# Two chunks' scores, then two chunks' sums, then products: another order of TensorE's work in a fused attention and expert layer

## The chip, the cores and the metric

The kernel runs on one core of one Trainium2 chip. The metric is the device time of one execution in microseconds (us). The kernel before took 775.37 us, the median of three runs (775.12 to 777.02).

The engines are named as in the profile: PE is TensorE (matrix products), PEld its weight loads, DVE is VectorE, ACT is ScalarE, POOL is GpSimd, SP issues most DMAs.

## What is computed

The input is x of 4 sequences (B) of 1024 positions (T) with 256 channels (C), all in float32. Two residual layers follow each other:

```python
x = x + attention(layernorm(x))   # 16 heads of 16, causal, with a slope per head (ALiBi)
x = x + ffn(layernorm(x))
```

The attention scores are `q @ k.T / 4 + slope * (key - query)` for keys up to the query, softmax over the keys, times v, then a projection. The second layer is, for each position, a small attention over the 4 sequences of the batch (16 heads of 16), a projection, a layer norm, a router that takes the higher number of the two best of 8 experts, that expert's two products with a GELU in between, and another layer norm.

## The kernel before

**Units, groups, rounds.** The attention works on units: a sequence with a chunk of 256 queries (chunks 0 to 2, twelve units), and a sequence with 128 queries for the last chunk (eight units: its first halves for all sequences, then its second halves). `begins` (L2147) says at which place each unit begins; `begins[B]`, the first unit behind the first chunk, is 8. A unit has 4 groups of 4 heads, and the keys of a group are taken in rounds of up to 512 columns (key block by queries). A round that holds the diagonal is narrower where keys are later than queries: 384 columns for the own round of a 256-query unit, and for the first halves of the last chunk, where the second round has three key blocks of four.

**A round** is scored by `score` (L986), later weighed by `weigh` (L1023). `score` multiplies keys by queries, 4 heads at once, in TensorE tiles of 32 rows (the profile's `sk<-slots`, 32*128); the result lies in two pairs of PSUM banks, two heads each. ScalarE takes the exp of each pair (L1007, `p<-sk`), so two exps to a round, into tiles of the pool `probs`, which has 7. The own round is then masked by GpSimd (L1017). `weigh` takes two rounds and multiplies values by these tiles, 4 heads at once, in tiles of 32 columns (`pv<-p,v`, 128*32), into one more pair of banks, which ScalarE copies out or VectorE adds to what is there (L1063, L1065). It also gives the sums of the softmax, by a column of ones, which is why the text calls this step "sums".

**PSUM.** There are four pairs of banks. `pair_of_banks` (L663) gives them out in turn: whatever takes a pair waits until the one that took it four calls earlier has been read. `bank` (L669) gives a single bank: a fresh pair's first half, then its second half, unless `pair_of_banks` was called in between.

**Products** are all other work of TensorE, in tiles of 128*128: transposes of the normalised input and projections to q, k and v of later units (`xtp`, `qkp`, `vp`), projections of finished units (`op`), and the second layer's products (`utp`, `qkvp`, `ctp`, `ao`, `place`) of fronts. A front (L1594) is a generator of the second layer for 128 positions of the 4 sequences; its stages are marked D (products), E, P (VectorE), N (ScalarE), R (GpSimd).

**Places.** The order of everything is written out by the loop at L2302. Rounds are taken by twos; a place p holds rounds 2p and 2p+1 and there are 80 places. In each, in this order: the first round's score; `E_slot` (L2248: work due at this half place, stores, loads, then the fronts' VectorE stages); `D_slot` (L2260: products due at this place, then fronts' products up to an estimated 10 us, with VectorE stages in between); `fill` (L2298: the loads of keys for a unit's group into `slots`, once the unit before is scored); more VectorE stages; the second round's score; `weigh` of the two rounds of the place before (`waiting`); `fill`; `E_slot` again. A planner keeps estimates of the time of each engine (`time`) and of each pair (`pair_free`), and lets a front's stage go only when it should be ready, so its estimates choose which place a product falls in. [...]

`at_E` puts work at a half place, `at_D` at a place. `prepare_biases` (L1488) splits biases into three bfloat16 pieces and stores each by a DMA; its last stage needs what `prepare_router(2)` leaves behind at place 11 (L2244).

Of the kernel before, what the change touches and what calls it, by code (L numbers as in the profile page):

```python
# [38 lines left out]
B, T, C = 4, 1024, 256  # L39
# [568 lines left out]
def fast_layer(ctx: ExitStack, tc: tile.TileContext, odd, x, wq, wk, wv, wp, w_in, w_out, w_r,  # L608
# [252 lines left out]
    sums, at = [], 0  # L861
# [13 lines left out]
    def issue_stores(*keys, age=None):  # L875
        due = [it for it in stores if it[0] in keys or age is not None and it[1] >= age]
        for it in due:
            stores.remove(it)
            it[2]()
# [77 lines left out]
    def fill_slots(u, g):  # L957

        n, i, _ = units[u]
        c, b = batches[n]  # L960
        if b == 0 and c and i == 0:
            query_rows(c, g)
        n_cols = W + (c + 1) * W
        issue_stores(("k", n, g // 2))
        src = k_of[b][4 * g * D:4 * (g + 1) * D, :n_cols]
        if c == 0:
            row_ = 4 * (g % 2) * D
            src = held["kq", n, g // 2][row_:row_ + 4 * D].rearrange("p k w -> p (k w)")
        queue = nc.scalar if u == 0 and g % 2 else nc.sync
        queue.dma_start(slots[g][0:P:2, :n_cols], src)  # L970
# [11 lines left out]
    def n_rounds(u):  # L982
        n, i, size = units[u]
        return -(-(batches[n][0] * PC + i + size) // (QC // (size * P)))
# [150 lines left out]
    for j in range(4):  # L1135
        at = slice(j * S, (j + 1) * S)
# [351 lines left out]
    def prepare_biases(stage):  # L1488

        if stage == 0:
            b1_rows = fact.tile([E, C], F32, tag="equal", name="b1_rows")
            nc.scalar.dma_start(
                b1_rows.rearrange("e (c p) -> e c p", p=P),
                b1.rearrange("p (e c) -> e c p", c=CC),
            )
            b2_rows = fact.tile([E, C], F32, tag="before", name="b2_rows")
            nc.scalar.dma_start(b2_rows, b2)
            b_row = fact.tile([1, 2 * C], F32, tag="u", name="b_row", bufs=2)  # L1500
            for k, at in enumerate((B_IN, B_OUT)):
                nc.scalar.dma_start(
                    b_row[:, k * C:(k + 1) * C], rows[at:at + C].unsqueeze(0)
                )
            held["biases"] = (
                (b1_rows, b_bf[0]), (b2_rows, b_bf[1]),
                (b_row[:, :C], in_bf), (b_row[:, C:], out_bf),
            )
            return
        src, three = held["biases"][stage - 1]  # L1510
        if three is out_bf:
            nc.vector.tensor_tensor(src, src, router["passed"][0:1, :C], ALU.add)
        n, width = src.shape
        rest = fact.tile([n, width], F32, tag="pr", name="rest")
        nc.vector.tensor_copy(rest, src)
        pieces = fact.tile([n, 3, width], BF16, tag="turned", name="pieces", bufs=TURNED)
        for k in range(3):
            nc.vector.tensor_copy(pieces[:, k], rest)
            nc.sync.dma_start(three[k * n:(k + 1) * n, :width], pieces[:, k])
            if k < 2:  # L1520
                nc.vector.tensor_tensor(rest, rest, pieces[:, k], ALU.subtract)
# [545 lines left out]
    def load_next():  # L2067
        while to_load and (
            to_load[0] < X_BUFS or left_x[(to_load[0] - X_BUFS) // B] == PC
        ):  # L2070
            load_x(to_load.pop(0))
# [5 lines left out]
    def busy(on, cost, ready=0.0):  # L2077
        time[on] = max(time[on], ready) + cost
        return time[on]

    def on_tensor(cost):
        return busy("PE", cost, max([0.0] + [pair_free[k] for k in taken]))
# [6 lines left out]
    def product(cost, what):  # L2089
        taken.clear()  # L2090
        what()
        end = on_tensor(cost)
        busy("DVE", OF_D * cost, end - 0.5 * cost)
        read_at(max(end + READ, time["DVE"]))
        return end

    def start_fronts():
        if queue and len(running) < 2:
            issue_stores(*[it[0] for it in stores if it[0][0] == "u"])
        while queue and len(running) < 2:  # L2100
            running.append(Running(queue.pop(0)))

    def take_E(some=True):

        start_fronts()
        left = some
        while left:
            left = False
            for it in list(running):
                now, kind = time["PE"], it.kind  # L2110
                if kind not in ("E", "N", "R", "P"):
                    continue
                on = {"E": "DVE", "P": "DVE", "N": "ACT"}.get(kind)
                if it.ready > max(now, time[on] if on else 0.0) + EARLY_BY:
                    continue
                if on == "DVE" and time["DVE"] > now + AHEAD:
                    continue
                if kind == "R":
                    it.ready = max(now, it.ready) + ROOT
                else:  # L2120
                    it.ready = busy(on, it.cost if on == "DVE" else 0.5, it.ready)
                left = True
                it.next()
                if it.kind == "end":
                    running.remove(it)

    def take_D(cost, some):

        for it in list(running):
            while it.kind[0] in "Dd":  # L2130
                if it.kind == "DQ" and ("qkv",) in held:
                    break
                if it.kind != "d" and it.ready > time["PE"] + EARLY_BY:
                    break
                if cost and cost + it.cost > D_SLOT:
                    break
                if it.kind == "DQ":
                    held["qkv",] = True
                cost += it.cost
                end = product(it.cost, it.next)  # L2140

                it.ready = max(end + READ, time["DVE"])
                take_E(some)
            if it.kind == "end" and it in running:
                running.remove(it)

    begins = [0]  # L2147
# [4 lines left out]
    def at_E(k, what, cost=0.0):  # L2152
        of_E.setdefault(k, []).append((cost, what))
# [7 lines left out]
    for u, (n, i, size) in enumerate(units):  # L2161
# [4 lines left out]
        if u == n:  # L2166
            if n > 2:
                at_E(2 * begins[n - 3], lambda n=n: to_load.append(n))
            for k in range(3):
                at = (-5, -5, -4)[k] if n == 1 else 2 * q - 7 + k  # L2170
# [37 lines left out]
    def pop_due(due, now):  # L2208
        some = sorted((it for it in due if it[0] <= now), key=lambda it: it[0])
        for it in some:  # L2210
            due.remove(it)
        return [(cost, what) for _, cost, what in some]
# [24 lines left out]
        at_E(1 + g, lambda g=g: key_rows(g, W, T, nc.vector if g else nc.gpsimd))  # L2237
    at_E(4, prepare)
    at_E(6, part.prepare)
    for k, at in enumerate((-6, 12, 13, 14, 23)):  # L2240
        at_E(at, lambda k=k: prepare_biases(k))
    at_D(9, 1.0, lambda: prepare_router(0))
    at_D(10, 1.5, lambda: prepare_router(1))
# [4 lines left out]
    def E_slot(k, some=True):  # L2248
        for cost, what in of_E.pop(k, []) + pop_due(due_E, time["PE"]):
            what()  # L2250
            busy("DVE", cost)
        issue_stores(age=1)
        for it in stores:
            it[1] += 1
        load_next()
        if tables and fetching:
            experts.fetch()
        take_E(some)

    def D_slot(p, some=True):  # L2260
        todo = of_D.pop(p, []) + pop_due(due_D, time["PE"])
        for cost, what in todo:
            product(cost, what)
        take_D(sum(cost for cost, _ in todo), some)
# [11 lines left out]
    def columns_of(u, r):  # L2276
        return sum(units[u][2] * P - off for _, off in blocks_of(u, r))

    def score_next(k):
        u, g, r = rounds[k]  # L2280
        taken.clear()
        waiting.append((u, g, r, score(u, g, r)))
        end, n = on_tensor(SWITCH + columns_of(u, r) * COLUMN), columns_of(u, r)
        for pair in list(taken):
            pair_free[pair] = busy("ACT", EXP_AT_ALL + 2 * n * EXP, end)
        if r == n_rounds(u) - 1 and u < last_unit:
            to_fill.append((u + 1, g))
# [10 lines left out]
    def fill():  # L2298
        while to_fill:
            fill_slots(*to_fill.pop(0))  # L2300

    for p in range(len(rounds) // 2):  # L2302
        then = p < len(rounds) // 2 - 1
        score_next(2 * p)
        E_slot(2 * p)
        D_slot(p, then)
        fill()
        take_E(then)
        score_next(2 * p + 1)
        if len(waiting) > 2:  # L2310
            weigh_next(waiting[:2])
            del waiting[:2]
        fill()
        E_slot(2 * p + 1, then)
    for _, what in pop_due(due_E, NEVER):
        what()
    weigh_next(waiting)
# [105 lines left out]
    while threads:  # L2423
# [4 lines left out]
        at, _, it = min((begin(it) + FIRST_BY * n, n, it) for n, it in enumerate(threads))  # L2428
# [124 lines left out]
```

## Time and profile before

| what | value |
|---|---|
| median of three runs | 775.37 us |
| the profiled execution | 776.72 us, of which the span from first to last instruction 774.9 us |
| granted clock of TensorE, mean | 0.97 |
| scoring: matmul records, busy | 3456, 178.5 us |
| weighing: matmul records, busy | 3456, 146.9 us |
| exps of scores: count, mean of one | 320 x 128 partitions, 940 ns |

A float32 product appears as two records. The loop of places runs from about 21 to 606 us, places 8 and up from about 78 us; the experts follow.

Further views that bear on the change are the waits of TensorE from 78 to 600 us: 4.5 us for VectorE's copies of `kq` (4 times), 4.0 us of the weighing for ScalarE's exps (11 times), 3.7 us of the scoring for exps (7 times), 3.5 us of `place` for VectorE (3 times). A row of such a view says who waited, for whom, the sum, how often and the longest. A row of the timeline says when a group of like instructions began, how long it lasted from its first start to its last end, engine, line, operation, output<-inputs, the shape, how many, and in brackets how long the engine stood before it and what ended that. Line 589 is a helper through which TensorE, VectorE and ScalarE are called, so groups are told apart by their tiles.

### The profile page before, as it was taken

How to read it: one execution, taken by the hardware profiler on the slowest of the kernel's cores; microseconds unless marked ns; L12 is line 12 of the kernel's file. 1: busy time of each engine (PE TensorE's matmuls, PEld its weight loads, DVE VectorE, ACT ScalarE, POOL GpSimd, SP SyncE). 2: the span in 40 equal slices, each digit the busy share in tenths (PEclk: the TensorE clock that was granted, in tenths of full speed). 3: DMA queues.
4: the chain of work that ended last, by engine and by line, in shares of the span. 5: the costliest groups of instructions: out<-in, count | busy, mean ns of one | idle time of the engine just before them, and what ended most of it. 6: DMA issues, size and time to landing. Idle time of an engine off the chain costs nothing. (4 is left out here: it accounts for less than half of the span.)

```text
span 774.9 us, 21884 instructions
## 1 busy us (share of the span) xinstructions
PE 696.7 (90%) x8945; PEld 525.6 (68%) x8945; DVE 514.0 (66%) x1266; ACT 425.9 (55%) x647; POOL 243.0 (31%) x345
## 2 busy tenths in 40 slices
PE   3989899999999999999989999999999687989991
PEld 2667577666666666575668877687778456878891
DVE  5447436477985765899672427698679778877462
ACT  1545547555465656556557656568558054546550
POOL 4644113221222221104221221123112330478873
PEclk9999999999999999999999999999999898999996
DMA  7535544431452432315354445345342670344421
GB/s 227 167 117 176 172 129 139 139 118 49 129 160 86 140 113 67 102 58 159 93 172 134 142 146 164 93 139 187 112 116 58 174 282 1 110 137 128 125 82 41
DMA packets 70872, 98.48 MB, mean 127 GB/s; under 512 B 15408, under 2 KB 54635, under 8 KB 70252
## 3 DMA queue, kind: packets, MB, share of 16 engines
q1 hardware_dynamic: 58528, 67.82, 28.4%
q10 hardware_dynamic: 7884, 16.05, 6.6%
q0 software_dynamic: 4352, 13.11, 5.6%
q8 instruction: 74, 1.21, 0.6%
q14 instruction: 34, 0.28, 0.1%
HBM read 60.50 MB, written 34.59 MB: 123 GB/s over the span
## 5 line engine op out<-in xcount | busy, mean ns | idle before, releaser
L589 ACT ACTIVATE p<-sk 128x1024 f32<-128x1024 f32 (+1 forms) x320 | 287.9, 940 | 148.4 <-PE sk L589 118.6
L1017 POOL TENSOR_SCALAR_AFFINE_SELECT p<-p 128x512 f32<-128x512 f32 (+1 forms) x160 | 106.6, 670 | 404.8 <-ACT p L589 402.5
L589 PE MATMUL sk<-slots 32*128 32x128 f32 (+1 forms) x3456 | 178.5, 325 | 10.1 <-DVE kq L589 4.7
L589 PEld LDWEIGHTS sk<-slots 32*128 32x128 f32 x3456 | 134.6, 187 | 53.5 <-issue 20.5
L589 PE MATMUL pv<-p,v 128*32 128x128 f32 (+1 forms) x3456 | 146.9, 317 | 9.6 <-ACT p L589 4.0
L589 PEld LDWEIGHTS pv<-p,v 128*32 128x32 f32 x3456 | 96.9, 111 | 48.8 <-issue 10.0
L589 PE MATMUL qkvp<-w_in,ut 128*128 128x264 f32 (+1 forms) x240 | 83.5, 486 | 0.2 <-ACT ut L589 0.2
L589 PEld LDWEIGHTS qkvp<-w_in,ut 128*128 128x128 f32 x240 | 42.5, 190 | 28.8 <-issue 24.3
L589 PE MATMUL qkp<-xt,wqk 128*128 128x256 f32 x224 | 56.4, 397 | 0.0
L589 DVE COPY kq<-qkp 128x512 f32<-128x512 f32 x28 | 19.1, 684 | 50.1 <-PE qkp L589 50.1
L589 PEld LDWEIGHTS qkp<-xt,wqk 128*128 128x128 f32 x224 | 41.5, 194 | 10.7 <-issue 3.3
L589 PE MATMUL hid<-mt,w 128*128 128x128 f32 x272 | 41.4, 289 | 2.6 <-ACT ge L589 1.7
L589 ACT ACTIVATE mt<-mtp,columns 128x128 f32<-128x128 f32 x68 | 27.4, 454 | 26.9 <-PE mtp L589 26.9
L589 ACT COPY qkv<-qkvp 128x512 f32<-128x512 f32 x28 | 16.4, 585 | 44.9 <-PE qkvp L589 44.7
L589 DVE TENSOR_TENSOR pv<-vr,sc 128x1024 f32<-128x1024 f32 x32 | 39.2, 1224 | 2.4 <-PE ctp L589 2.1
L1868 POOL DMA_INDIRECT given<-rows,rows x34 | 37.4, 1100 | 9.0 <-issue 7.9
L589 DVE COPY vr<-qkvp 128x264 f32<-128x264 f32 x28 | 12.1, 431 | 42.1 <-PE qkvp L589 42.1
L589 PEld LDWEIGHTS hid<-mt,w 128*128 128x128 f32 x272 | 37.2, 198 | 3.9 <-ACT ge L589 2.2
L589 DVE TENSOR_REDUCE sc<-pr 128x64 f32<-128x1024 f32 x32 | 39.0, 1220 | 1.1
L589 DVE TENSOR_TENSOR pr<-qkv 128x1024 f32<-128x1024 f32 x32 | 39.2, 1224 | 0.5 <-ACT qkv L589 0.2
L1983 POOL DMA_INDIRECT out_dram<-o,out_rows x34 | 34.6, 1018 | 7.4 <-issue 5.0
L589 PE MATMUL oe<-w,ge 128*128 (+1 forms) x136 | 36.8, 395 | 0.0
(320 smaller groups left out, 1005.1 us busy)
## 6 DMA issues: line engine op xcount, KB each, us to landing
slots<-k SPq DMA_DIRECT2D x32, 320.0 KB
k<-kq SPq DMA_DIRECT2D x32, 256.0 KB
v<-v ACTq DMA_DIRECT2D x4, 1152.0 KB
x<-in_x_dram SPq DMA_DIRECT2D x16, 256.0 KB
y<-yt SPq DMA_DIRECT2D x16, 256.0 KB
rows<-x SPq DMA_DIRECT2D x32, 128.0 KB
slots<-k SPq DMA_DIRECT2D x16, 256.0 KB
rows<-u SPq DMA_DIRECT2D x8, 512.0 KB
```

What stands on the lines that cost most here:

```text
L589: ins = made(*args, **kwargs)
L1017: nc.gpsimd.affine_select(blocks, blocks, pattern=[[0, 2], [0, size], [1, P]], compare_op=ALU.is_ge, fill=0.0, base=0, channel_multiplier=-1,)
L1868: nc.gpsimd.indirect_dma_start(out=self.hx, out_offset=None, in_=t.rows_of, in_offset=bass.IndirectOffsetOnAxis(ap=t.rows_[:, self.j:self. ...
L1983: ins = nc.gpsimd.indirect_dma_start(out=out.rearrange("t n c -> (t n) c"), out_offset=bass.IndirectOffsetOnAxis(ap=t.table.out_rows[:, t. ...
```

## The change

From place 8 on (`between` is false) the order in a place is: first score, `fill`, `E_slot`, second score, `fill`, `weigh`, `E_slot`, `D_slot`, VectorE stages. In places 0 to 7 the order stays. The last stage of `prepare_biases` moves from half place 23 to 25, since place 11's products now come behind both its half places.

```diff
-    for k, at in enumerate((-6, 12, 13, 14, 23)):
+    for k, at in enumerate((-6, 12, 13, 14, 25)):
         at_E(at, lambda k=k: prepare_biases(k))
...
     for p in range(len(rounds) // 2):
         then = p < len(rounds) // 2 - 1
+        between = p < begins[B]
         score_next(2 * p)
+        if not between:
+            fill()
         E_slot(2 * p)
-        D_slot(p, then)
-        fill()
-        take_E(then)
+        if between:
+            D_slot(p)
+            fill()
+            take_E()
         score_next(2 * p + 1)
+        if not between:
+            fill()
         if len(waiting) > 2:
             weigh_next(waiting[:2])
             del waiting[:2]
-        fill()
+        if between:
+            fill()
         E_slot(2 * p + 1, then)
+        if not between:
+            D_slot(p, then)
+            take_E(then)
```

## The prediction, made before the changed kernel was run

> **What bounds the kernel now.** I read the engine rows first, then busy time by stretch, then who waited for whom on TensorE, and last the timeline of TensorE.
>
> ```profile
> PE 696.7 (90%) x8945; PEld 525.6 (68%) x8945; DVE 514.0 (66%) x1266; ACT 425.9 (55%) x647; POOL 243.0 (31%) x345
> ...
> 78.00:190.00 112.00, 108.35 (x1088) 74.76 (x1084) 60.34 (x132) 60.87 (x88) 24.13 (x32) 0.98 0.41 126
> 190.00:390.00 200.00, 191.04 (x2127) 128.37 (x2119) 153.42 (x344) 117.83 (x156) 44.33 (x49) 0.98 0.35 108
> 390.00:505.00 115.00, 109.94 (x2053) 86.51 (x2053) 59.42 (x141) 70.65 (x101) 22.31 (x39) 0.99 0.47 144
> 505.00:600.00 95.00, 90.80 (x2082) 74.84 (x2075) 79.42 (x193) 65.48 (x84) 21.06 (x35) 1.00 0.40 123
> ```
>
> From 78 to 600 us, which is nearly all that the change touches, TensorE works some 96% of the time; VectorE reaches 77% in the second stretch and 84% in the fourth, ScalarE at most 69%. So in the attention part the order of instructions on TensorE sets the time, and each gap on it counts in full. The clock column (0.98 to 1.00) stays out of it. The remaining 175 us (experts) hold none of the reordered loop.
>
> One stretch of TensorE's timeline shows both kinds of place side by side:
>
> ```profile
> 417.74 1.84 PE L589 MATMUL sk<-slots 32*128 32x128 f32 x56
> ...
> 419.00 3.35 ACT L589 ACTIVATE p<-sk 128x1024 f32<-128x1024 f32 x4 [0.79 <-PE sk L589]
> 420.08 1.74 PE L589 MATMUL pv<-p,v 128*32 128x128 f32 x56 [0.50 <-ACT p L589]
> ...
> 421.75 1.17 PE L589 MATMUL sk<-slots 32*128 32x128 f32 x32
> ...
> 422.85 1.99 PE L589 MATMUL qkp<-xt,wqk 128*128 128x256 f32 x8
> ...
> 424.77 0.95 PE L589 MATMUL sk<-slots 32*128 32x128 f32 x24
> ...
> 425.65 1.74 PE L589 MATMUL pv<-p,v 128*32 128x128 f32 x56
> ...
> 427.32 1.17 PE L589 MATMUL sk<-slots 32*128 32x128 f32 x32
> ```
>
> sk is scoring, pv weighing, all else (here qkp) a product. At 421.75 stands a place as today: first score, product, second score, sums. At 417.74 stands a place with **no product due**: its scores (32+24 records) already run back to back, then the sums. That is exactly the order that the change gives to every place, so before already shows its price: the sums start 2.34 us after the first score (417.74 to 420.08), with TensorE idle for 0.50 us because ScalarE has not yet emptied the first pair of banks. The cause is in the code. There are four pairs, taken in turn. Two scores take all four, so weigh() gets the first score's first pair again and must wait for its exp: that starts 1.26 us after the score (419.00) and takes about 0.97 us. With a product in between, weigh() gets the product's pair, or one further on.
>
> **The sum, part by part.** Counting the places from 8 on (72 of the 80) in TensorE's timeline: 59 have products, 13 have none. These 13 keep their order and cost what they cost now.
>
> *Scores and sums (the path).* First score plus second score, start to next start, in places without a stall: 1.08+0.87 = 1.95 us in the second chunk (512 score columns, then 384), 1.10+0.88 = 1.98 in the fourth chunk's first half, 1.10+1.10 = 2.20 in its second half (512, 512). After, by the places that have no product: 2.32, 2.34 and 2.34. In the third chunk all three pairings occur: 512/384 goes from 1.95 to 2.32; 512/512 from 2.16 to 2.32; 384/512 from 1.95 to about 1.96 (an exp over 768 starts 1.05 us after its score and takes 0.81; with 0.1 us to the sums, 1.96). Times the counts:
> second chunk 15 x 0.37 = 5.6; third 8 x 0.37 + 5 x 0.16 + 8 x 0.01 = 3.9; fourth 12 x 0.36 + 11 x 0.14 = 5.9. **Together +15.4 us.** The saving in tilings is already inside these differences.
>
> *Tilings, and two rules.* The Trainium skill, "TensorEngine Tiling (Array Packing)", Key Properties, says that changing the tiling mode drains TensorE. The trace agrees: the 56 score records start in groups of four 0.112 us apart, so 14 groups are 1.56 us and 8 are 0.89, where the 8 groups from 421.75 take 1.10: 0.21 us for entering and leaving. By that rule alone two scores in one block save about 0.2 us: 59 x 0.2 = 12 us gained. The same page, PSUM Bottleneck, speaks against the change: tiling speeds up TensorE, not the emptying of PSUM, which may become the limit. Here it does: the two scores could be followed at about 1.79 us, and the exp allows 2.34. I take the row, +15.4. The switch from sums straight to a product is nowhere in before; leaving the sums for a score costs 1.67 - 14 x 0.109 = 0.14 us. Between 0 and twice this, 59 places move by -8 to +8; I take it unchanged.
>
> *Stalls that vanish.* Where the product is tiny, the second score stands today for the exp of the first, four times (235, 370, 577, 597 us) or is pulled apart by the switch (526): against 2.2 their score pairs cost 0.7 to 1.8 more. Two scores in a row do not have these waits: **-5 us**.
>
> *Products end directly before two scores.* The last pair of a product is needed again four pairs later. Today that is the next place's first score, after a score and the sums, 2.7 us behind the product. After, it is the next place's second score, 0.9 us behind it (1.3 us before it costs anything, as the sums wait anyway). VectorE empties most products, in order behind the fronts' work:
>
> ```profile
> 403.57 0.19 DVE L589 TENSOR_TENSOR hot<-low_con,expert 128x32 bf16<-128x32 f32 x1
> 403.68 0.68 DVE L589 COPY kq<-qkp 128x512 f32<-128x512 f32 x1
> ...
> 404.42 0.93 PE L589 MATMUL sk<-slots 32*128 32x128 f32 x16 [2.10 <-DVE kq L589]
> ```
>
> Here the product ended at 399.70 and was copied out by 404.36, 4.7 us late. Reading the end of the last copy of every product in the timeline: 21 of the 59 end more than 1.3 us after it, in sum 27 us over. Some 9.5 us of such waits exist today, so with the same lateness +17 us; if the longer places give VectorE the time to catch up, 0. Its queue is fed after the sums as it is fed today after the first score, so nothing makes it earlier, but a wait on TensorE drains it: I take the middle, **+8**.
>
> *The rest.* take_E and E_slot are called as often as before, so VectorE's and GpSimd's work is the same in number. An exp of a front (`sc<-sc`) waiting for VectorE holds ScalarE's queue ahead of the score's exp, which is now on the path: six or seven fronts, under 0.5 us each, **+2**. fill() moves ahead of E_slot and D_slot: 60 loads of slots (0.49 us of SP each), the stores of k that they push out, and query_rows at two chunk ends (0.35 + 0.41 us of VectorE, eight times) are issued 1 to 5 us earlier; on SP they already wait for scores, and the rows are read four or more places (over 20 us) later: 0, or some 3 us if VectorE stands for a score. The last biases (three small DMAs on SP, six VectorE operations) go from half place 23 to 25, one place after the product they need; first used near 208 us, they are there by 125: 0. Fronts get further while the places are longer, which may take **-1 us** from the tail.
>
> Sum: 15.4 - 5 + 8 + 2 - 1 = +19 us on the profiled execution's 776.7 us (span 774.9 and 1.8 around it), 796. The median, 775.4, lies 1.3 lower: **794 us**. A measurement of this kernel tells 0.3% (2.3 us) from no change.
>
> **Rivals.**
> 1. *The tiling decides* (faster): if the exp's wait were hidden, a place would go from 1.98 to 1.79 us: 59 x 0.19 = -11, 764 us. For it: the drain is real, and a free switch from sums to product adds to it. Against it: 13 of 13 places without a product show the wait. It decides only if the wait stays under 0.19 us, or if the waits standing today around products (score pairs 20 us over their base, sums 9.5) vanish by more than the 15.4. Chance 0.09.
> 2. *Gains and waits cancel*: 15.4, less 5 of vanishing stalls, less 8 for a free switch into the products: +2, 777 us, with late copies at 0. Needs three terms at one end. Chance of within 0.3%: 0.04.
> 3. *VectorE's copies become the bound*: lateness unchanged (+17), a dearer switch (+8): 15.4 + 17 + 8 + 2 - 5 = +37, 813 us. For it: VectorE at 77% in the third chunk (190 to 390 us), where most late copies lie. Against it: a standing TensorE lets that queue run empty. Chance of more than 810: 0.07.
> The forecast, slower by 4 to 35 us, holds 0.80. That the order does not change is excluded: the pairs go by the order of calls.
>
> **How the numbers follow.** Range 779 to 810: +4 is the sum with the switch at its low end and late copies at 1; +35 is rival 3 nearly whole. Below lie 0.13 (rivals 1 and 2), above 0.07. Faster 0.09, same 0.04, slower 0.87.
>
> **What would show it.** In the profile after: TensorE's wait of sums for p by ScalarE rises from 4 us in 11 cases (78 to 600 us) to some 20 to 30 us in over 50; first score to sums 2.3 us in places with a product too; PE's busy time about equal and its share lower; waits of the second score for VectorE's kq, vr, u or ct. Wrong, if sums start less than 2 us after a full first score, or if a switch into products is far from 0.14 us.

## The result, and the profile after

The changed kernel takes **805.8 us** (median of 4 runs, 805.36 to 807.25), where the kernel before takes 775.75 us beside it (4 runs): ratio **1.0383** [1.0356, 1.041], slower by about 30 us. The profiled execution has a span of 803.4 us, against 774.9.

The engine rows of the page after (busy time, share of the span, instructions), then TensorE's waits from 78 to 600 us (who waited for whom: us in all, times, longest):

```profile
PE 695.7 (87%) x8945; PEld 535.0 (67%) x8945; DVE 511.5 (64%) x1266; ACT 417.4 (52%) x647; POOL 236.1 (29%) x345
```

```profile
PE pv L589 <- ACT p L589: 22.6, 44, 3.2
PE sk L589 <- DVE x L589: 6.3, 3, 2.8
PE qkp L589 <- DVE ctx L589: 3.4, 2, 3.2
```

TensorE has the same number of instructions and the same busy time as before (695.7 and 696.7 us), and a span 28.5 us longer. The weighing's wait for ScalarE's exps, 4.0 us in 11 cases before, is now 22.6 in 44 (20 to 30 us in over 50 cases were forecast). Busy time by stretch (TensorE first, in us; then PEld, DVE, ACT, POOL; the granted clock; DMA share; GB/s) shows that in the loop the clock is not it, and that TensorE's share fell in each stretch:

```profile
78.00:190.00 112.00, 102.70 (x1046) 73.44 (x1038) 56.97 (x131) 55.89 (x84) 22.32 (x31) 0.97 0.40 123
190.00:390.00 200.00, 182.43 (x1995) 127.43 (x1997) 154.50 (x341) 107.76 (x146) 38.81 (x46) 0.98 0.34 106
390.00:505.00 115.00, 107.13 (x1931) 82.89 (x1925) 56.36 (x139) 68.83 (x99) 20.37 (x37) 1.00 0.45 142
505.00:600.00 95.00, 89.90 (x2033) 73.87 (x2032) 68.52 (x181) 62.86 (x83) 19.20 (x35) 1.00 0.41 129
```

TensorE's timeline after, at one place with a product in front of it:

```profile
427.64 1.03 PE L589 MATMUL qkp<-xt,wqk 128*128 128x256 f32 x4
...
428.60 1.84 PE L589 MATMUL sk<-slots 32*128 32x128 f32 x56
...
429.87 3.35 ACT L589 ACTIVATE p<-sk 128x1024 f32<-128x1024 f32 x4 [2.43 <-PE sk L589]
...
430.94 1.74 PE L589 MATMUL pv<-p,v 128*32 128x128 f32 x56 [0.50 <-ACT p L589]
```

The product (qkp) stands ahead of the two scores, the scores run as one block of 56 records, and the sums begin 2.34 us after the first score (428.60 to 430.94) having stood 0.50 us for the exp: the row that the prediction took from a place without a product, now in a place with one.

**Where the 28.5 us are.** I cut the trace at three points: the start of the last sums of the loop, and the first and the last matmul of `counts_all`, the count of tokens for each expert, behind which the bulk of the experts' work stands in TensorE's order. The count has five matmuls: one adds the fronts up to front 6 (`so_far`), four add front 7 (`hot`).

| stretch | before | after | difference |
|---|---|---|---|
| start to last sums | 603.5 | 620.6 | +17.1 |
| last sums to the count's first matmul | 72.9 | 83.9 | +11.0 |
| first matmul to the count done | 0.3 | 7.6 | +7.3 |
| count done to end | 98.2 | 91.3 | -6.9 |

The loop costs about what was forecast. The +11.4 us behind it were not foreseen. These rows of TensorE's timeline are of before (first fence) and after (second), from the last sums to the count:

```profile
603.51 1.96 PE L589 MATMUL pv<-p,v 128*32 128x128 f32 x64 [2.39 <-DVE yn L589]
...
615.03 1.72 PE L589 MATMUL ctp<-ident,ctx 128*128 128x128 f32 x8
...
631.37 0.19 PE L589 MATMUL place<-hot,lower 128*128 128x32 bf16 x1 [1.40 <-DVE hot L589]
...
676.41 0.17 PE L589 MATMUL counts_all<-so_far,ones_bf 128*128 128x8 bf16 x1
676.44 0.24 PE L589 MATMUL counts_all<-hot,ones_bf 128*128 128x8 bf16 x4
```

```profile
620.63 1.95 PE L589 MATMUL pv<-p,v 128*32 128x128 f32 x64
...
640.36 0.52 PE L589 MATMUL ctp<-ident,ctx 128*128 128x128 f32 x3
...
689.15 0.18 PE L589 MATMUL place<-hot,lower 128*128 128x32 bf16 x1
...
704.54 0.17 PE L589 MATMUL counts_all<-so_far,ones_bf 128*128 128x8 bf16 x1
711.88 0.25 PE L589 MATMUL counts_all<-hot,ones_bf 128*128 128x8 bf16 x4 [7.17 <-DVE hot L589]
```

`ctp` and `place` here belong to front 6, the last front that begins inside the loop (the last front of all, 7, runs behind it). Counted from the last sums, its transposes of the context stand at +11.5 us before and +19.7 after, and its `place` at +27.9 and +68.5: after, it is served so late that work of experts and of front 7 comes between. The count begins 11 us later, then stands 7.17 us for front 7's `hot` on VectorE, and is done 18.3 us later (73.2 and 91.5 us behind the last sums). Part of this comes back: between the last sums and the count TensorE has done 11 of the experts' pieces (one piece is a tile of tokens through its expert's two products, about 2.7 us of TensorE) instead of 7, so 23 instead of 27 are left behind it, and the part behind it is 6.9 us shorter. The net is the +11.4.

### The profile page after: what moved, and what is told of

Its sections match the earlier page's. It is cut to its first block, busy times and chain, and to the rows that moved or that the text cites. A ratio compares the mean times of both kernels' runs of the same rounds, so it can differ in the third digit from the quotient of the medians.

```text
span 803.4 us, 21919 instructions
## 1 busy us (share of the span) xinstructions
PE 695.7 (87%) x8945; PEld 535.0 (67%) x8945; DVE 511.5 (64%) x1266; ACT 417.4 (52%) x647; POOL 236.1 (29%) x345
## 5 line engine op out<-in xcount | busy, mean ns | idle before, releaser
L589 ACT ACTIVATE p<-sk 128x1024 f32<-128x1024 f32 (+1 forms) x320 | 277.7, 943 | 154.9 <-PE sk L589 135.6
L1017 POOL TENSOR_SCALAR_AFFINE_SELECT p<-p 128x512 f32<-128x512 f32 (+1 forms) x160 | 100.9, 634 | 437.1 <-ACT p L589 435.2
L589 PE MATMUL sk<-slots 32*128 32x128 f32 (+1 forms) x3456 | 168.2, 322 | 15.5 <-DVE x L589 6.3
L589 PEld LDWEIGHTS sk<-slots 32*128 32x128 f32 x3456 | 138.2, 188 | 46.8 <-issue 13.3
L589 PEld LDWEIGHTS pv<-p,v 128*32 128x32 f32 x3456 | 98.7, 112 | 65.3 <-ACT p L589 28.5
L589 PE MATMUL qkvp<-w_in,ut 128*128 128x264 f32 (+1 forms) x224 | 77.5, 483 | 0.0
L589 PEld LDWEIGHTS qkvp<-w_in,ut 128*128 128x128 f32 x224 | 40.5, 193 | 26.9 <-issue 22.6
L1868 POOL DMA_INDIRECT given<-rows,rows x34 | 38.0, 1118 | 21.8 <-DVE at_t L589 12.8
L589 ACT COPY qkv<-qkvp 128x512 f32<-128x512 f32 x24 | 14.1, 587 | 50.4 <-PE qkvp L589 50.4
```

What stands on the lines that cost most here:

```text
L589: ins = made(*args, **kwargs)
L1017: nc.gpsimd.affine_select(blocks, blocks, pattern=[[0, 2], [0, size], [1, P]], compare_op=ALU.is_ge, fill=0.0, base=0, channel_multiplier=-1,)
L1868: nc.gpsimd.indirect_dma_start(out=self.hx, out_offset=None, in_=t.rows_of, in_offset=bass.IndirectOffsetOnAxis(ap=t.rows_[:, self.j:self. ...
```

## The experiments

Two theories were to be tested. **Loop:** the sums stand for the exp of the first score's first pair, in the places from 8 on. **Tail:** where front 6 stands when the loop ends. The table has every run in the order of the text: its median with the ratio to the kernel before in the same set of runs, and four readings of its own trace: when the last sums start, and the time from there to the first matmul of the count, to the count done, and to the end. The kernel before itself has medians of 775.75, 786.84, 782.27, 776.75 and 776.46 us in the five sets, so times are compared by ratio, and places in the loop by trace.

| run | median, us | ratio | last sums | to the count | count done | to the end |
|---|---|---|---|---|---|---|
| before (the first profile) | 775.75 | 1 | 603.5 | 72.9 | 73.2 | 171.4 |
| after (the first profile) | 805.8 | 1.0383 [1.0356, 1.041] | 620.6 | 83.9 | 91.5 | 182.8 |
| e5_new_until_48 | 797.19 | 1.0096 [1.006, 1.0132] | 616.1 | 72.4 | 72.7 | 180.7 |
| e6_new_from_48 | 796.92 | 1.0115 [1.006, 1.017] | 612.7 | 83.8 | 91.4 | 184.6 |
| e12_new_until_64 | 807.71 | 1.039 [1.0344, 1.0436] | 623.9 | 84.5 | 92.1 | 184.0 |
| e1_after_early | 808.55 | 1.0268 [1.024, 1.0296] | 629.7 | 78.9 | 79.2 | 180.9 |
| e2_before_early | 793.89 | 1.0092 [1.0059, 1.0125] | 608.4 | 74.6 | 74.9 | 185.2 |
| e7_after_again | 806.32 | 1.0293 [1.0235, 1.0352] | 620.6 | 84.9 | 92.5 | 184.6 |
| e8_before_again (one run) | 782.5 | | 601.4 | 70.8 | 71.0 | 179.1 |
| e3_after_split | 811.31 | 1.0355 [1.0276, 1.0433] | 625.5 | 85.0 | 92.6 | 185.0 |
| e4_before_split | 785.18 | 1.0033 [1.0, 1.0066] | 604.8 | 72.3 | 72.6 | 176.9 |
| e9_after_short | 815.0 | 1.0485 [1.045, 1.052] | 609.3 | 83.5 | 91.1 | 204.1 |
| e10_before_short | 795.92 | 1.0253 [1.0214, 1.0291] | 601.2 | 72.2 | 72.5 | 192.1 |
| e11_before_sums_first | 786.46 | 1.0131 [1.0105, 1.0157] | 614.0 | 71.6 | 71.9 | 170.6 |

### Which chunk makes the tail

The new order for a part of the places. The edit in the changed kernel, for the second and third chunk alone (e5), and for the fourth chunk alone (e6):

```diff
-        between = p < begins[B]
+        between = p < begins[B] or p >= begins[3 * B]      # e5
+        between = p < begins[3 * B]                        # e6
```

> The new order in places 8 to 47 alone (second and third chunk), the old one from 48. Theory (the loop loses by the first score's exp, 9.5 us in these two chunks; the 11 us behind the loop are lost because the front that begins last in the loop stands further back when it ends, which the fourth chunk's order sets): 775.4 + 9.5 + 1 = 786 us, and from the last sums to the end 171 us as before. Rival (any new order costs the tail its 11 us): 797 us, 183 us behind the loop.

> The new order from place 48 on alone (fourth chunk). Theory: the loop loses 5.9 us and about 1 us of late copies, the tail 11 us: 793 us, with 182 to 183 us behind the last sums. Rival (the tail's loss goes with the loop's total delay, of which this is a third): 775.4 + 7 + 4 = 786 us.

The loop's loss splits: last sums at 616.1 and 612.7 us, 12.6 and 9.2 later than before, 21.8 together against 17.1 for both at once. The count does not split. In e5 it is done 72.7 us behind the last sums, as in the kernel before (7 pieces of the experts ahead of it); in e6 91.4, as in the changed kernel (11 pieces). So the late count comes with the order in the fourth chunk, and a longer loop by itself does not bring it: e5's is 12.6 us longer.

The whole time behind the last sums, by which both forecasts were stated, fits less well: 180.7 us in e5, nearer to its rival's 183 than to the theory's 171, and 184.6 in e6. e5's excess lies behind the count (108.0 us, before 98.2), and e8 below, the kernel before itself, has it too (108.1). By ratio the halves cost 1.0% and 1.2%, together less than the changed kernel's 3 to 4%. e5's 1.0% is nearer to the theory (786 of 775.4 us, 1.4%) than to its rival (2.8%), but e6's 1.2% is nearer to its rival (1.4%) than to the theory (2.3%). So the two halves show where the late count comes from, not what it costs.

### What in the fourth chunk: its last places, or where front 6 stands

In the emitted order, front 6 takes its stage in front of `qkvp` at place 73 before, and at place 75 after. It cannot begin until unit 15 is projected; that projection runs at 540.7 us before and 559.3 after. The planner dates it by the end of unit 15's weighing, which its estimates put 13.5 us later in the new order, and the new order asks for the products due only behind both scores and the sums of a place. The following kernel separates this from what happens in the last places themselves: these run in the old order, but the planner still lets front 6 go late, at place 76.

```diff
-        between = p < begins[B]
+        between = p < begins[B] or p >= begins[3 * B] + 16
```

> The changed kernel with the new order for the places 8 to 63 only; the last 16 places run in the old one. In the emitted order of this kernel, front 6 (the last that begins in the loop) begins its matmuls with wqk's successors at place 76 of 80, against 75 in the changed kernel and 73 in the kernel before, because the sums of unit 15 fall 13.5 us later in the planner's time as in the changed kernel. Theory (the 11 us behind the loop come from where front 6 stands in the instruction streams, not from the order within the last places): from the last sums to the experts' count it takes 80 to 88 us, as in the changed kernel (84), although the last 16 places have the old order. Rival (the order within the last places leaves VectorE with more work at the loop's end): 71 to 74 us, as in the kernel before. Loop by the counts of the prediction: new order costs all but the fourth chunk's second half, so the last sums start at 615 to 620 us.

The last 16 places have the old order, and to the count it is still 84.5 us (done at 92.1):

```profile
620.53 5.39 PE L589 MATMUL pv<-p,v 128*32 128x128 f32 x128
...
699.05 0.19 PE L589 MATMUL place<-hot,lower 128*128 128x32 bf16 x1 [0.98 <-DVE hot L589]
...
708.40 0.17 PE L589 MATMUL counts_all<-so_far,ones_bf 128*128 128x8 bf16 x1
715.75 0.25 PE L589 MATMUL counts_all<-hot,ones_bf 128*128 128x8 bf16 x4 [7.18 <-DVE hot L589]
```

Front 6's `place` comes even later (75.1 us behind the start of the last sums, 623.9, which lies inside the first row's group) and the count with it, with the same wait of 7.18 us in it. The theory holds for the count, and its rival falls. The forecast of the loop, 615 to 620 us, was missed by 4: the places 64 to 79 took 105.9 us in the old order, 102.9 in the changed kernel.

### Bringing front 6 forward

Unit 15's sums, reciprocals and projection are made due sooner, in the changed kernel (e1) and in the kernel before (e2):

```diff
                 by = HURRIED.get(by, NEVER)
+            if u == (NC * B) - 1:
+                by = {SUMS_BY: 2.0, INVERTED_BY: 5.5, Y_BY: 7.5, DIVIDED_BY: 14.0}[by]
             due_E.append((at + by, cost, lambda what=what: what(u)))
         by = NEVER if u == last_unit - 1 else PROJECTED_BY
+        if u == (NC * B) - 1:
+            by = 15.0
```

> The changed kernel, but the last first-half unit (15) of the fourth chunk is divided and projected 14 and 15 us of the planner's time behind its sums instead of 26 and 28, so that the front that waits for it begins earlier. Theory (that front's unfinished stages cost the tail its 11 us): its transposes begin in the loop some 10 us earlier, the time behind the last sums falls from 183 to about 172 us, the whole to 795 us. Rival (the tail is longer for another reason, such as a later last unit): 804 to 806 us.

> The kernel before, with the same earlier division and projection of unit 15. Theory (the stage of that front at the loop's end sets the tail): it gains here too, since two of its four last weighted sums and its norm stand in the tail today: 3 to 8 us, 767 to 772 us. Rival (in the old order the last front and the experts alone set the tail): 775 us, no change.

In the changed kernel the count is done 79.2 us behind the last sums instead of 91.5, and front 6's `place` moves from +68.5 to +30.9: the count follows front 6, by 12 of the 18 us. The time to the end hardly does: 180.9 us behind the last sums, where the theory said about 172 and the rival 183, and where the changed kernel has 182.8 and 184.6. And the loop pays: the last sums start at 629.7, 9 us later. In the kernel before nothing is gained at all (count done at 74.9 against 73.2, loop 5 us longer), and that expectation was missed too: a front's work has to be done somewhere, and inside the loop it stands in front of scores. The planner's dates are a balance that moving one of them did not improve.

### The same two kernels again

Both unchanged, on the chip of e3 and e4 (that of the first profiles is not on record), to see which readings repeat. e8 is a single run; its 782.5 us lie close to the 782.27 of the kernel before in its set.

> The changed kernel as it is, for a trace on the chip of the other runs of this call. 1.038 of the kernel before; the last sums at 620 us, 83 to 84 us from them to the count of all positions' experts. If chips differ, the difference stands behind that count.

> The kernel before as it is, for a trace on the chip of the other runs of this call: the last sums at 603 us, 73 us from them to the count of all positions' experts, as in the first trace.

Last sums at 620.6 and 601.4 us, count done 92.5 and 71.0 behind them: the longer loop and the late count repeat. The price of the late count does not: to the end it is 184.6 against 179.1 us, +5.4 instead of +11.4, because the kernel before now takes 108.1 us behind the count where it took 98.2 (the changed kernel 92.1 and 91.3). The ratio is accordingly smaller here, 1.0293.

### The exp on the path: longer

The first score's first pair has its exp in two instructions, one for each bank, with the weighing told to wait for the first alone. For the changed kernel in each place from 8 on (e3), for the kernel before in the 13 places without a product (e4):

```diff
-            nc.scalar.activation(
-                pt[:, :, :width], ps[pair][:, :, :width], AF.Exp, scale=1.0 / math.sqrt(D)
-            )
+            for j in (0, 1) if halved and not pair else (slice(0, 2),):
+                last_half = nc.scalar.activation(
+                    pt[:, j, :width], ps[pair][:, j, :width], AF.Exp, scale=1.0 / math.sqrt(D)
+                )
...
+                    if other:
+                        tc.declare_no_dep(ins.ins, other, reason="another bank of the pair")
```

> The changed kernel, but from place 8 on the exp of the first score's first pair goes by banks, in two instructions, and the sums that take this pair wait for the first bank alone, which is the one they write. Theory (the 15 us of the loop are this wait): the sums start about 1.95 us after a full first score instead of 2.34 (1.26 to the exp, 0.57 for half of it, 0.1), 2.05 where both scores are full; 72 places gain 0.3 to 0.4 us, 24 us in all, against 0.2 us more of ScalarE in each place: 0.97 of the changed kernel's time, about 782 us of 806. The tail keeps its 11 us. Rival (the loop's loss lies in copies that come late or in the switch from sums to products): under 5 us gained.

> The kernel before, with the same split of one exp in the 13 places behind the first chunk that have no product (12, 24, 36, 42, 52, 56, 61, 62, 66, 67, 69, 70, 76) and so have the two scores in a row already. Theory: 13 times 0.3 to 0.4 us, 4 to 5 us: 771 us for 775.4, 0.994. Rival (ScalarE, with four exps of 0.97 us and a copy, is the limit in these places of 4.0 us, so that 0.2 us more of it take the gain back): within 1 us of before.

The edit did not do what it was meant to: the sums still wait for both halves. In e3's timeline they begin 2.41 us after the first score (435.18 to 437.59), though the first half of the exp was done 1.87 us after it (436.45 + 0.60):

```profile
435.18 1.84 PE L589 MATMUL sk<-slots 32*128 32x128 f32 x56
...
436.45 0.60 ACT L589 ACTIVATE p<-sk 128x512 f32<-128x512 f32 x1 [0.50 <-PE sk L589]
436.94 2.92 ACT L589 ACTIVATE p<-sk 128x512 f32<-128x512 f32 x4
...
437.59 1.74 PE L589 MATMUL pv<-p,v 128*32 128x128 f32 x56 [0.56 <-ACT p L589]
```

So a release by bank was not tried, in e3 or in e4, where nothing was gained (1.0033 for 0.994 expected). What e3 did try is an exp that ends 0.06 us later: in 72 places this makes 4.3 us, and the last sums start 4.9 us later than in the unsplit kernel beside it (625.5 against 620.6). That agrees with the loop theory with its sign turned: what the exp takes, each place takes.

### The exp on the path: shorter

The exp of each first score's first pair covers half of the columns, from place 8 on, in both orders. GpSimd writes 1.0 into the other half, so these softmax weights and the routing that follows from them are not the reference's; only the loop is compared.

```diff
+            some = width // 2 if short and not pair else width
             nc.scalar.activation(
-                pt[:, :, :width], ps[pair][:, :, :width], AF.Exp, scale=1.0 / math.sqrt(D)
+                pt[:, :, :some], ps[pair][:, :, :some], AF.Exp, scale=1.0 / math.sqrt(D)
             )
+            if some < width:
+                nc.gpsimd.memset(pt[:, :, some:width], 1.0)
...
-        waiting.append((u, g, r, score(u, g, r)))
+        waiting.append((u, g, r, score(u, g, r, k % 2 == 0 and k >= 2 * begins[B])))
```

> The changed kernel, in which from the second chunk on (72 places) the exp of each first score's first pair covers only half of the columns; GpSimd writes 1.0 into the other half of the tile, so that the softmax weights of those columns, and with them the routing behind, are not the reference's. Theory (the sums stand in every place for the exp that empties the first score's first pair): that exp takes about 0.57 instead of 0.97 us, the sums follow the first score at some 1.95 to 2.05 us instead of 2.34, and the loop's last sums start 72 x 0.3 to 0.4 = 22 to 28 us earlier than the 620.6 us of the changed kernel, at 593 to 599 us. Rival (the loop's loss of 17 us lies elsewhere: in copies of products, in the switch from sums to product): under 5 us, last sums at 616 us or later. The part behind the loop depends on the routing and is not compared.

> The same shortened exp in the kernel before the change. Theory: only the 13 places without a product (and the four or five tiny products) stand for this exp, so the last sums start 13 x 0.35 = 5 to 7 us earlier, at 595 to 598 us instead of 601 to 603; the two orders then end the loop within some 5 us of each other, the new one no longer behind by 17. Rival (a shorter exp helps both orders alike because ScalarE's queue is what is short): both gain the same 20 us or more.

One place of e9 in the timeline, then TensorE's waits of e9 from 78 to 600 us:

```profile
429.58 1.84 PE L589 MATMUL sk<-slots 32*128 32x128 f32 x56
...
430.85 2.92 ACT L589 ACTIVATE p<-sk 128x512 f32<-128x512 f32 x4 [2.43 <-PE sk L589]
...
431.50 1.74 PE L589 MATMUL pv<-p,v 128*32 128x128 f32 x56
```

```profile
PE sk L589 <- DVE x L589: 7.2, 4, 3.5
PE qkp L589 <- DVE ctx L589: 3.4, 2, 3.2
PE sk L589 <- ACT p L589: 3.4, 2, 2.9
PE place L589 <- DVE hot L589: 2.4, 2, 1.3
PE sk L589 <- DVE rank L589: 1.7, 2, 0.9
PE pv L589 <- ACT p L589: 1.5, 4, 1.0
```

The sums follow the first score at 1.92 us (429.58 to 431.50), the weighing's wait for the exp fell from 22.6 to 1.5 us, and the last sums start at 609.3 instead of 620.6. The sign and the place of the effect are the theory's; the rival's bound (616 or later) is passed. But 11.3 us were gained where 22 to 28 were expected. More than the wait itself was never to be had, and from the sums in place 9 to the last sums that is 19.8 us in the changed kernel. Over this stretch it falls by 17.6 us; TensorE's other waits grow by 4.7 (19.5 to 24.2), most of them for VectorE's copies of products (x, rank, vr, yn) and for `place`; its busy time grows by 2.1, with the granted clock at 0.50 for 20.5 us instead of 13.7. **The exp's wait was covering part of the late copies**; shorten the exp, and they are on the path.

The kernel before gains little, as expected of the theory and not of its rival: place 79's sums start at 594.8 us instead of 599.2, but the last sums only at 601.2, against 601.4 to 603.5, since they stand 4.41 us for `yn`. With an exp that hardly holds either order, the new one is still 8.1 us behind (609.3 against 601.2), and the expectation that they end within some 5 us of each other was missed. TensorE's waits explain 2.4 us of this (26.4 and 24.0 over the same stretch); the rest is busy time (487.9 and 481.5 us), with the granted clock at 0.50 for 20.5 us in e9 and for 6.8 in e10.

### Sums between two scores

The converse repair, in the kernel before: where no product stands between the scores, the sums go there.

```diff
         take_E(then)
+        early = p >= begins[B] and n_pairs[0] == scored and not early
+        if early:
+            weigh_next(waiting[:2])
+            del waiting[:2]
         score_next(2 * p + 1)
```

> The kernel before, with one change: in a place from the second chunk on in which no product stands between the two scores, the sums go between them (first score, sums, second score), unless the place before did so too. Theory: those places lose their wait for the exp (0.37 us, less in the fourth chunk's second half) and pay one more change of tiling (0.14 to 0.21 us): some 10 places by 0.2 to 0.3 us = 2 to 3 us earlier end of the loop, 0.3% faster, ratio 0.996 to 0.998. Rival (the sums, now earlier, stand for the second score's exp and mask of the place before): no gain, ratio 0.999 to 1.003.

It is slower, by 1.3%. Up to 590 us it neither gains nor loses much (place 63's sums at 496.8 us against 496.9), since the wait only moves into the next place:

```profile
530.92 1.17 PE L589 MATMUL sk<-slots 32*128 32x128 f32 x32
532.02 1.96 PE L589 MATMUL pv<-p,v 128*32 128x128 f32 x64
...
533.91 2.07 PE L589 MATMUL sk<-slots 32*128 32x128 f32 x64
...
536.25 0.49 PE L589 MATMUL sk<-slots 32*128 32x128 f32 x4 [0.28 <-ACT p L589]
537.16 1.16 PE L589 MATMUL sk<-slots 32*128 32x128 f32 x28 [0.42 <-ACT p L589]
```

Between the sums at 532.02 and those at 538.25 stand three scores in a row (64, 4 and 28 records), which need six pairs where there are four; they stand for exps twice, 0.28 and 0.42 us. Then, near the loop's end, one score stands 6.96 us for `who_f`, a front's result on VectorE that was not in the way before. The rival's reason (a wait in the neighbouring place) is right; its size is not, because of that stall.

No version that was run beats the kernel before.

## Why the prediction was right or wrong

The time, 805.8 us, is 11.8 over the 794 forecast, inside the range and on the forecast side. By its steps:

- **Scores and sums, +15.4: right.** The sums start 2.32 us after a first score in the second chunk and 2.34 in both halves of the fourth (medians), product or not, as the rows had said. From the sums in place 9 to the last sums the loop takes 15.8 us longer: TensorE's wait of the sums for the exp grows by 15.8 (4.0 to 19.8), its other waits by 1.7, and its busy time falls by 1.7, with the granted clock at 0.50 for 13.7 us in both. The loop's parts became longer by 4.9 us in the second chunk (forecast 5.6), 6.0 in the third (3.9) and 6.1 in the fourth (5.9), read between the sums of the places 7, 23, 47 and 79. These carry the small terms too. The rule on PSUM that was weighed against the rule on the drain decided the sign: e9 takes most of the loss back by shortening the exp.
- **The switch from sums to a product, unchanged: right.** Sums of 896 columns to the next start cost 1.65 to 1.67 us, whether a product or a score follows; there was no free gain there, on which rival 2 rested.
- **Vanishing stalls, -5: not realised.** TensorE's stalls around products sum to about 30 us before and 31 after. The old ones went, others came: at place 79 a score stands 3.8 us for `yn`.
- **Late copies, +8: mis-sized, near +2.** Copies that end more than 1.3 us behind the product sum to about 11 us over in the trace after, where it was 27 before; less the 9.5 us of such waits that stood before, that is near +2. The working had said that waits on TensorE drain VectorE's queue; fewer copies are late, as it said, and the exp's wait covers part of what is left, as e9 shows. The two terms are not cleanly apart, since the stalls around products hold waits for late copies.
- Together these small terms were to give +5 with the front's exp; the loop's +17.1 leaves about 2 for them. The loop was forecast at +20.
- **"Fronts get further while the places are longer, which may take -1 us from the tail": this step failed.** The time behind the last sums grew by 11.4 us in the first pair of profiles and by 5.4 in the second. Longer places do not carry fronts further: front 6 waits for unit 15's projection, which the planner dates by its own clock and which the new order asks for only behind the sums of a place. It was let go two places later, and e5, e6 and e12 tie the late count (18 to 21 us) to that; some of it comes back, since more of the experts' work is then done before the count. How much time the late count costs is not shown: e1 took back 12 of its 18 us and only 2 to 4 us of the time to the end, and e1 moved the loop as well.

Of the rivals, the tiling that decides and the cancelling terms fell with the exp's wait. VectorE's copies as the bound came near in time (813) for another reason than its own: the late copies shrank, and the tail made up the sum.

**Luck:** the forecast lay 11.8 us low, and the term behind it, the tail, had the wrong sign; the range of 31 us took it in. **Open:** the time behind the count. The kernel before took 98.2 us there in the first profile and 108.1 in e8. Until TensorE's last product its granted clock was 0.50 for 3.4 us in the one and for 13.7 in the other, which is worth some 5 of the 10 us (an estimate: 10.3 us at half speed); why the clock fell more, and the other 5 us, were not tried.

## What to carry to other kernels

Before two steps are joined to save a change of tiling, count the buffers that they take together: if the joined steps take all of them, the step behind waits for the reader of the first, and a place that already runs so by chance shows the price. Where a planner with estimated times chooses the order, a change in one loop also moves what it lets go near the loop's end; the first item there that gates the next phase has to be followed through the emitted order, place by place, up to where its result is whole: here the count began 11 us later but was done 18 us later. A wait that was removed is worth only what the next-latest waits leave of it: here 11.3 of 19.8 us.

## What was unexpected of the hardware

- An exp over two banks (1024 columns) takes 1.02 us and over half of them 0.60, so the two halves cost more than the whole; the second half starts 0.49 us after the first (436.45 to 436.94), and the pair was done 0.06 us later.
- The same kernel kept its loop within about 2 us from one set of runs to another (last sums at 603.5 and 601.4; 620.6 both times), while the part behind the count of the kernel before differed by 10 us.
